# Attention scores of the last three row blocks of a four-layer graph network: from an element-wise product to a small matmul

## The chip, the cores and the metric

The kernel runs on one core of one Trainium2 chip. The metric is the device time of one execution in microseconds (us). TensorE (PE) does matmuls, VectorE (DVE), ScalarE (ACT) and GpSimd (POOL) work element by element, and SyncE (SP) issues most of the DMAs. Each engine runs its own instructions in the order of its own queue, and waits on semaphores for the others.

## The reference, cut to what matters

A graph of 2708 nodes with 512 features passes through four layers, each of the form x = x + layer(relu(layernorm(x)), adj). Layers 0, 1 and 3 aggregate over neighbours with the adjacency matrix. The change lies in layer 2, a graph attention layer with 8 heads of 64 outputs:

```
Wh = einsum('nd,hdo->hno', x, W)          # W: 8 x 512 x 64
f1 = einsum('hno,ho->hn', Wh, a1)
f2 = einsum('hno,ho->hn', Wh, a2)
e  = leaky_relu(f1[:, :, None] + f2[:, None, :], 0.2)
e  = where(adj > 0, e, -9e15)
h' = einsum('hnm,hmo->hno', softmax(e), Wh)
out = elu(h')
```

So every node has 16 scores: for each head the product of its 64 values Wh with a1 and with a2. Because Wh is itself x times W, a score is also x times a vector of 512 numbers: the sum over o of W[h, d, o] * a1[h, o].

## The kernel before

The nodes are cut into 22 chunks of 128 rows (R = 128, NC = 22; the last has 20 rows). All matmuls concerned are in fp32. All PSUM tiles come from one pool of eight banks, `ps`.

**Layer 1's aggregation** (`aggregate`, L433) runs over seven spans of chunks (4, 4, 4, 4, 3, 2 and 1 of them), and for each over the 22 blocks m of neighbours. For each pair, VectorE makes one tile of weights `kt` (`weight1`, L871, the instruction of L873), four units ahead of the matmuls (L425) that use it; `kt` has five buffers. In the middle of each span `before1` (L901) is called for each chunk c of the span, to load its rows.

**Layer 2's dense stage** is a pipeline over the chunks (`dense`, L271; `staged`, L251). For each chunk: load, normalize, transpose by TensorE into `hT` (L246, evicted by ScalarE at L248), then `product2` (L1104):

- TensorE multiplies `hT` with `w2s`, the weights of all heads, into `wh_ps` (L187; L200 for the last chunk), ScalarE copies it to `wh` (L1112, L1110), and SyncE stores it to DRAM (`whd`, L101).
- VectorE multiplies `wh` with the row of a1, GpSimd with the row of a2 (both L1117, output `wh_a`, four buffers). GpSimd then adds the upper half of each head's 64 products to the lower half (L1123).

One step later `sums2` (L1127) sums both products over o with two VectorE reductions (L1134), placed behind the next chunk's first product, and a VectorE instruction of 16 columns clamps the scores to +-31 and writes them to `f12` (L1136). The last stage, `rows2` (L1191), takes the scores of the first 11 chunks (in two groups) through exponentials and to DRAM as rows (`exps_nodes`, L1152, gives `er`; `exps2`, L1155, gives `ef` and `ec`; `row2`, L1145), and starts the attention: the broadcast row `rb` is loaded (L983) and the first weights are made.

**Attention** is a list of steps (unit, m); a unit is a head, or half the columns of the first and of the last head. Each step needs a tile `t` that VectorE makes from `rb`, `ec` and the adjacency (`make`, L1060, the instruction of L1070; four buffers, three steps ahead of use) and a tile `whs` that ScalarE scales (`scale`, L1045; L1054 and L1056; four buffers, three steps ahead too). TensorE then runs 16 matmuls into `av` and, where needed, 8 into `sums` (both L1318). A plan written out by hand (`behind`, L1423) adds to each step what else is due: the scores of chunks 11 to 21 through `exps_nodes` and `exps2` at step 4, their rows (TensorE transposes them into `f_ps` at L1147, ScalarE copies at L1149 and issues the store itself at L1150) from step 4 on, ScalarE's casts of the adjacency to bf16 (`mask`, L1382, tile `x`), TensorE's neighbour counts that use them (`count_neighbors`, L1394, `adj_sums`), small tiles for the 20 last rows (`load_tails`, L995), and the next layer's weights `wfs` and `wfn` (`load_l3_weights`, L1416), which take the two buffers of the pool `weights` that `w2s` and the score vectors `arows` (L1099) hold before.

The order of each engine's queue comes from a scheduler that merges these streams; `issue_after` places one instruction behind another.

Of the kernel before, what the change touches and what calls it, by code (L numbers as in the profile page):

```python
# [8 lines left out]
F32 = mybir.dt.float32  # L9
# [6 lines left out]
ALU = mybir.AluOpType  # L16
AX = mybir.AxisListType
# [3 lines left out]
P = 128  # L21

R = 128
# [15 lines left out]
F_MAX = 30.0  # L39
# [5 lines left out]
def fast_layers(  # L45
# [36 lines left out]
    nc = tc.nc  # L82
    N, D = x_in.shape
    H, _, O = w2.shape
    NC = -(-N // R)
    NF = D // P
# [5 lines left out]
    def rows(c):  # L92
        return min(R, N - c * R)

    def move(engine, dst, src):

        if dst.shape[0] == last_rows:
            cut = last_rows // 16 * 16
            engine.dma_start(dst[:cut], src[:cut])
            return engine.dma_start(dst[cut:], src[cut:])  # L100
        return engine.dma_start(dst, src)  # L101
# [8 lines left out]
    KMAX = max(sizes)  # L110
# [7 lines left out]
    const = ctx.enter_context(tc.tile_pool(name="const", bufs=1))  # L118
    small = ctx.enter_context(tc.tile_pool(name="small", bufs=4))
    weights = ctx.enter_context(tc.tile_pool(name="weights", bufs=2))  # L120
    dram = ctx.enter_context(tc.tile_pool(name="dram", bufs=1, space=DRAM))

    common = ctx.enter_context(tc.tile_pool(name="common", bufs=2))

    ps = ctx.enter_context(tc.tile_pool(name="ps", bufs=8, space=PSUM, reuse_waits="tile"))

    ident = const.tile([P, P], F32, name="ident")
    make_identity(nc, ident)
    oneb = const.tile([P, 32], BF16, name="oneb")
    nc.gpsimd.memset(oneb, 1.0)  # L130
    ones = const.tile([P, 1], F32, name="ones")
# [45 lines left out]
    def load_row(pool, src, name, into=None):  # L177

        t = into
        if t is None:  # L180
            t = pool.tile([P, D], F32, name=name)
        nc.sync.dma_start(t, bass.AP(tensor=src.tensor, offset=src.offset, ap=[[0, P], [1, D]]))
        return t
# [24 lines left out]
    def any_product(c, po, lhsT, w, n):  # L208
        if c == NC - 1:
            product_of_last(po, lhsT, w)  # L210
        else:
            product(po, lhsT, w, n)
# [106 lines left out]
    def load_x(src, c, name="x", pool=None, bufs=XBUFS, twice=False, tag=None, rows_of=natural):  # L319
        n = rows(c)  # L320
        t = (pool or common).tile([P, D], F32, name=name, tag=tag or name, bufs=bufs)
        if twice and c == NC - 1:
            nc.gpsimd.memset(t[:R], 0.0)
            move(nc.sync, t[TAIL : TAIL + n, :], rows_of(src, c))
        loads[c] = move(nc.sync, t[:n], rows_of(src, c)).ins
        return t
# [85 lines left out]
    def pattern(m, cs, n=R):  # L412

        g, k = where[m]
        v = vT[g][:n, k, cs[0] * R : (cs[-1] + 1) * R]
        return v.rearrange("p (c r) -> p c r", r=R)

    def by_chunk(t, cs):
        return t[:, : len(cs) * R].rearrange("p (c r) -> p c r", r=R)
# [56 lines left out]
    with ExitStack() as ring_ctx:  # L476
# [390 lines left out]
        w2s = weights.tile([P, NF, H, O], F32, name="w2s", tag="w")  # L867
        for f in range(NF):
            nc.sync.dma_start(w2s[:, f], w2[:, f * P : (f + 1) * P, :].rearrange("h p o -> p h o"))

        def weight1(m, cs):  # L871
            kt = wk.tile([R, WG], F32R, name="kt", bufs=5)
            nc.vector.scalar_tensor_tensor(  # L873
                by_chunk(kt, cs),
                lastr[:, cs[0] * R : (cs[-1] + 1) * R].rearrange("p (c r) -> p c r", r=R),
                index[:R, m : m + 1],
                pattern(m, cs),
                op0=ALU.is_ge,
                op1=ALU.mult,
            )  # L880
            return kt
# [17 lines left out]
        wmax = const.tile([P, 2], F32, name="wmax")  # L899

        def before1(c):  # L901
            if c == 2 * KMAX:
                for i, op in enumerate((ALU.max, ALU.min)):
                    nc.vector.tensor_reduce(
                        wmax[:, i : i + 1], w2s.rearrange("p f h o -> p (f h o)"), AX.X, op
                    )
            return load_x(x1, c)

        stages2 = dense(
            x2,  # L910
            lambda *args: product2(*args),
            False,
            [(3, lambda c: save_last2(c)), (4, lambda c: sums2(c)), (6, lambda c: rows2(c))],
            scalar=True,
        )
        ahead = [(m, emit_step, step, NC, stages2) for step, m in enumerate(AHEAD)]
        aggregate(weight1, h1, before1, after1, lead=4, ahead=ahead)


# [39 lines left out]
    f12 = late.tile([P, NC, 2 * H], F32, name="f12")  # L959
# [136 lines left out]

    l2p = ctx.enter_context(ExitStack())
    pp = l2p.enter_context(tc.tile_pool(name="l2p", bufs=2, side="right", reuse_waits="tile"))
    arows = weights.tile([P, NF, D], F32, name="arows", tag="w")  # L1099
    ar = [load_row(None, a, None, into=arows[:, i]) for i, a in enumerate((a1, a2))]  # L1100

    products, firsts = {}, {}

    def product2(c, xc, hT, n):  # L1104
        po = ps.tile([P, D], F32, name="wh_ps", tag="ps")
        any_product(c, po, hT, w2s.rearrange("p f h o -> p f (h o)"), n)
        wh = pp.tile([R, D], F32, name="wh", bufs=3)
        if c == NC - 1:
            for own in corners:
                nc.scalar.copy(wh[:n, own[1]], po[own])  # L1110
        else:
            nc.scalar.copy(wh[:n], po[:n])  # L1112
        move(nc.sync, whd[c * R : c * R + n, :], wh[:n])
        for i in range(2):
            t = products[c, i] = pp.tile([R, H, O], F32, name="wh_a", bufs=4)
            eng = nc.gpsimd if i else nc.vector
            ins = eng.tensor_tensor(  # L1117
                t[:n].rearrange("p h o -> p (h o)"), wh[:n], ar[i][:n], ALU.mult
            )
            if i == 0:  # L1120
                firsts[c] = ins.ins
            else:
                nc.gpsimd.tensor_tensor(  # L1123
                    t[:n, :, : O // 2], t[:n, :, : O // 2], t[:n, :, O // 2 :], ALU.add
                )

    def sums2(c):  # L1127
        n = rows(c)
        f = small.tile([P, 2, H], F32, name="f")

        with tc.issue_after(firsts[min(c + 1, NC - 1)]):
            for i in range(2):
                t = products.pop((c, i))
                nc.vector.tensor_reduce(f[:n, i, :], t[:n, :, : O // (1 + i)], AX.X, ALU.add)  # L1134

        nc.vector.tensor_scalar(  # L1136
            f12[:n, c, :],
            f[:n].rearrange("p i h -> p (i h)"),
            F_MAX + 1.0,
            -F_MAX - 1.0,  # L1140
            op0=ALU.min,
            op1=ALU.max,
        )

    def row2(c):  # L1145
# [4 lines left out]
        nc.scalar.dma_start(rT[:, c * R : (c + 1) * R], r)  # L1150

    def exps_nodes(cs):  # L1152
        nc.scalar.activation(er[:, cs], f12[:R, cs, :H], AF.Exp, scale=1.0 - SLOPE2)

    def exps2(cs):  # L1155
# [35 lines left out]
    def rows2(c):  # L1191
        for first, end in early_rows:
            if c == end - 1:
                exps_nodes(slice(first, end))
            for n in range(2):
                if first <= first + 2 * (c - end + 1) + n < end and c >= end - 1:
                    row2(first + 2 * (c - end + 1) + n)
        if c == EARLY - 1:
            exps2(slice(0, EARLY))
        if c == EARLY + 1:  # L1200
            load_row1(*units[0])
            split(0, EARLY)

        if c == LATE:
            load_wh(0)
            load_wh(GROUP)
        if LATE < c <= LATE + 3:
            scale(len(made))
            make(len(made))
# [213 lines left out]
    def behind(s, fn, *args):  # L1423
        plan.setdefault(s, []).append((fn, args))

    behind(4, exps_nodes, slice(EARLY, NC))
    behind(4, exps2, slice(EARLY, NC))
    for c in range(EARLY, NC):
# [755 lines left out]
def kernel(tc: tile.TileContext, *args: bass.AP):  # L2184

    nc = tc.nc
    with tc.tile_pool(name="verdict", bufs=1) as pool:
        verdict = pool.tile([1, 1], I32, name="verdict")
        fast_layers(tc, *args, verdict)
        odd = nc.values_load(verdict[0:1, 0:1], min_val=0, max_val=P + 1)  # L2190
        with tc.If(odd > 0):
            general_layers(tc, *args)
# [32 lines left out]
```

## Time and profile before

| what | value |
|---|---|
| time, three runs | 1741.11, 1741.48 and 1742.69 us; median 1741.48 |
| the profiled execution | 1741.66 us, of which the span from first to last instruction is 1739.8 us |
| TensorE busy | 1716.4 us (99% of the span) |
| VectorE, ScalarE, GpSimd busy | 75%, 49%, 14% |
| granted TensorE clock | 1.00 throughout |
| layer 1's aggregation | first matmul at 507.9 us |
| layer 2's dense stage | 725.4 to 810.1 us |
| attention's first matmul | 810.1 us |

A line of the timeline gives start, duration, engine, source line, operation, and output<-inputs; a number in brackets is the idle time of that engine just before, and what ended it. In the lines of windows each engine's busy time in the stretch stands with its number of instructions. An fp32 matmul shows as two records on TensorE. Matmuls overlap in their pipeline, so that the distance from one start to the next says more than a record's own duration.

### The profile page before, as it was taken

How to read it: one execution, taken by the hardware profiler on the slowest of the kernel's cores; microseconds unless marked ns; L12 is line 12 of the kernel's file. 1: busy time of each engine (PE TensorE's matmuls, PEld its weight loads, DVE VectorE, ACT ScalarE, POOL GpSimd, SP SyncE). 2: the span in 40 equal slices, each digit the busy share in tenths (PEclk: the TensorE clock that was granted, in tenths of full speed). 3: DMA queues.
4: the chain of work that ended last, by engine and by line, in shares of the span. 5: the costliest groups of instructions: out<-in, count | busy, mean ns of one | idle time of the engine just before them, and what ended most of it. 6: DMA issues, size and time to landing. Idle time of an engine off the chain costs nothing.

```text
span 1739.8 us, 29452 instructions
## 1 busy us (share of the span) xinstructions
PE 1716.4 (99%) x11280; PEld 1078.0 (62%) x11280; DVE 1309.3 (75%) x1902; ACT 846.7 (49%) x1556; POOL 248.5 (14%) x252
## 2 busy tenths in 40 slices
PE   8999999999999999999999999999999999999998
PEld 4567777744458888644575676434434455588886
DVE  7759889855555556888899999999999777633334
ACT  5446767622210000266878888888885666400000
POOL 1003323311111111366000000000001222100000
PEclk9999999999999999999999999999999999999999
DMA  8446666444551111332420220122022444313221
GB/s 288 140 124 195 204 207 190 141 116 123 123 142 49 49 49 49 117 129 99 118 79 15 61 64 26 47 65 63 16 69 70 142 140 130 106 40 106 74 73 41
DMA packets 167227, 177.37 MB, mean 102 GB/s; under 512 B 84127, under 2 KB 106591, under 8 KB 166060
## 3 DMA queue, kind: packets, MB, share of 16 engines
q1 hardware_dynamic: 144428, 131.99, 27.3%
q10 hardware_dynamic: 18808, 33.37, 5.1%
q0 software_dynamic: 3840, 10.03, 1.5%
q8 instruction: 90, 1.47, 0.4%
q14 instruction: 61, 0.50, 0.1%
HBM read 111.64 MB, written 55.36 MB: 96 GB/s over the span
## 4 chain that ended last, share of the span: by engine, by line
PE 87%; DVE 7%; ACT 2%; DMA 1%; issue 1%; SPq 1%; POOL 0%; ACTq 0%; DVEq 0%; POOLq 0%
PE acc L425 37%; PE av L1318 19%; PE nb_ps L187 8%; PE sums L1318 5%; PE h_ps L187 4%; PE self_ps L187 4%; PE line_ps L187 4%; DVE t L1070 4%; PE hT_ps L246 2%; PE fused_ps L371 2%; PE wh_ps L187 1%; DVE wh_a L1117 1%; PE av_ps L1253 1%; ACT b L1088 1%; DVE f L1134 1%
## 5 line engine op out<-in xcount | busy, mean ns | idle before, releaser
L1070 DVE SCALAR_TENSOR_TENSOR t<-rb,ec,vT 128x2708 f32<-128x2708 f32 (+2 forms) x214 | 510.7, 2447 | 8.1 <-PE sums L1318 6.3
L1318 PE MATMUL av<-t,whs 128*32 128x451 f32 (+5 forms) x4432 | 444.0, 513 | 5.9 <-DVE t L1070 4.6
L425 PE MATMUL acc<-halves,kt 128*128 128x512 f32 x1848 | 423.6, 390 | 1.0 <-DVE kt L873 1.0
L425 PEld LDWEIGHTS acc<-halves,kt 128*128 128x128 f32 x1848 | 346.0, 188 | 75.3 <-DVE kt L873 2.6
L1088 ACT ACTIVATE b<-t,eb 128x2708 bf16<-128x2708 f32 (+1 forms) x119 | 285.1, 2396 | 32.9 <-DVE t L1070 32.7
L1318 PEld LDWEIGHTS av<-t,whs 128*32 128x32 f32 (+1 forms) x4432 | 194.2, 110 | 163.1 <-issue 113.1
L425 PE MATMUL acc<-halves,ar 128*128 128x512 f32 x924 | 243.6, 414 | 0.0
L425 PEld LDWEIGHTS acc<-halves,ar 128*128 128x128 f32 x924 | 172.6, 188 | 58.2 <-issue 20.8
L223 ACT ACTIVATE ln_rs<-ln_mv,eps 128x1 f32<-128x1 f32 x88 | 25.8, 295 | 308.8 <-DVE ln_mv L221 307.3
L873 DVE SCALAR_TENSOR_TENSOR kt<-lastr,index,vT 128x512 fp32r<-128x512 int16 (+3 forms) x154 | 112.7, 746 | 72.3 <-PE acc L425 72.1
L1542 DVE CAST kt<-vT 128x512 fp32r<-128x512 uint8 (+3 forms) x154 | 56.3, 367 | 130.8 <-PE acc L425 130.7
L1270 POOL TENSOR_SCALAR z<-y 128x512 f32<-128x512 f32 x22 | 44.2, 2009 | 632.1 <-DVE y L1263 632.1
L558 DVE TENSOR_TENSOR_SCAN cum<-ai,deg 128x512 int16<-128x512 int32 (+2 forms) x110 | 128.1, 1168 | 0.0
L601 ACT ACTIVATE cum<-cum,limit 128x512 int16<-128x512 int16 (+3 forms) x132 | 88.0, 667 | 51.9 <-DVE deg L566 49.7
L1318 PE MATMUL sums<-t,whs 128*32 128x325 f32 (+4 forms) x952 | 103.5, 446 | 0.0
L1054 ACT ACTIVATE whs<-wh,ef 128x64 f32<-128x64 f32 x214 | 72.4, 341 | 53.4 <-PE av L1318 19.1
L219 DVE BATCH_NORM_STATS2 ln_st<-x 128x6 f32<-128x512 f32 x88 | 60.4, 688 | 48.6 <-DMA x<-x 34.4
L1318 PE MATMUL sums<-b,parts 128*32 128x338 bf16 (+2 forms) x884 | 77.1, 308 | 0.0
L187 PE MATMUL wh_ps<-w2s,hT 128*128 128x512 f32 x168 | 75.9, 594 | 0.6 <-ACT hT L248 0.6
L187 PE MATMUL h_ps<-w0s,hT 128*128 128x512 f32 x168 | 75.8, 594 | 0.1
L187 PE MATMUL self_ps<-wfs,hT 128*128 128x512 f32 x168 | 75.7, 593 | 0.0
L552 ACT ACTIVATE ar<-ai 128x512 fp32r<-128x512 int32 (+2 forms) x132 | 74.9, 568 | 1.4 <-DMA ai<-in_adj 0.9
(211 smaller groups left out, 1951.3 us busy)
## 6 DMA issues: line engine op xcount, KB each, us to landing
x<-x SPq DMA_DIRECT2D x105, 256.0 KB
ai<-in_adj SPq DMA_DIRECT2D x84, 256.0 KB
x<-x ACTq DMA_DIRECT2D x84, 256.0 KB
x<-in_x SPq DMA_DIRECT2D x42, 256.0 KB
rb<-rT SPq DMA_DIRECT2D x7, 1354.0 KB
wh<-whd SPq DMA_DIRECT2D x63, 96.0 KB
packed<-two POOLq DMA_DIRECT2D x44, 128.0 KB, 3.3
whd<-wh SPq DMA_DIRECT2D x21, 256.0 KB
```

The lines of the kernel that those rows point to most:

```text
L187: nc.tensor.matmul(po[:n], lhsT[:, f, :n], w[:, f, :], start=(f == 0), stop=(f == NF - 1))
L219: nc.vector.bn_stats(st[:n], xc[:n])
L425: nc.tensor.matmul(acc[:R], weight[:, k * R : (k + 1) * R], parts[:, i, :], start=(m == 0 and i == 0), stop=(m == NC - 1),)
L552: nc.scalar.activation(ar[:, :gw], ai[:, :gw], AF.Square, accum_out=squares[:R, m, g : g + 1])
L558: nc.vector.tensor_tensor_scan(cum[:n, :gw], ai[:n, :gw], ai[:n, :gw], 0.0 if g == 0 else deg[:n, m : m + 1], op0=ALU.add, op1=ALU.max,)
L601: nc.scalar.activation(cum[:n, :gw], cum[:n, :gw], AF.Sign, bias=limit[:n], scale=-1.0, accum_out=signs[:n, m, g : g + 1],)
L873: nc.vector.scalar_tensor_tensor(by_chunk(kt, cs), lastr[:, cs[0] * R : (cs[-1] + 1) * R].rearrange("p (c r) -> p c r", r=R), index[:R, m ...
L1054: ins = nc.scalar.activation(t[:q, :O], wh.pop((u, m))[:q], AF.Copy, scale=by)
L1070: ins = nc.vector.scalar_tensor_tensor(t[:q, : hi - lo], row[h][:q, lo:hi], ec[:q, m, h : h + 1], vT[g][:q, k, lo:hi], op0=ALU.max, op1=AL ...
L1088: nc.scalar.activation(b[:q, : hi - lo], weight[s][:, : hi - lo], AF.Sigmoid, bias=eb[:q, m, h : h + 1], scale=STEEP,)
L1318: nc.tensor.matmul(p[j * S : (j + 1) * S, : b - a], lhsT, rhs[:, part * size + a : part * size + b], start=(s % NC == 0), stop=(s % NC == ...
L1542: nc.vector.tensor_copy(by_chunk(kt, cs), pattern(m, cs))
```

## The change

- `arows` is loaded before layer 1's aggregation rather than at the start of layer 2.
- During layer 1's aggregation eight calls `fold(j)`, one from each of `before1(4)` to `before1(11)`, multiply `w2s` of one block of 128 input features with a1's or a2's row and sum over o, both on VectorE. This gives `w2a`, 512 x 16.
- For chunks 19, 20 and 21 (`DIRECT = NC - 3`) the scores are `hT` times `w2a`: four matmuls of 16 columns into a PSUM tile `fd_ps`, and one VectorE clamp from there to `f12`. The two products, GpSimd's addition and the two reductions fall away for them.
- For chunks 0 to 18 the reductions write to `f12` directly, and the clamp is done in place once for each group of chunks, in `exps_nodes`: chunks 0 to 5, 6 to 10, and 11 to 18.

```diff
+    w2a = const.tile([P, NF, 2 * H], F32, name="w2a")
...
+        arows = weights.tile([P, NF, D], F32, name="arows", tag="w")
+        ar = [load_row(None, a, None, into=arows[:, i]) for i, a in enumerate((a1, a2))]
+
+        def fold(j):
+            i, f = divmod(j, NF)
+            t = common.tile([P, D], F32, name="folded", tag="t", bufs=3)
+            nc.vector.tensor_tensor(
+                t, w2s[:, f].rearrange("p h o -> p (h o)"), ar[i], ALU.mult
+            )
+            nc.vector.tensor_reduce(
+                w2a[:, f, i * H : (i + 1) * H],
+                t.rearrange("p (h o) -> p h o", h=H),
+                AX.X,
+                ALU.add,
+            )
...
         def before1(c):
+            if KMAX <= c < KMAX + 2 * NF:
+                fold(c - KMAX)
...
-    arows = weights.tile([P, NF, D], F32, name="arows", tag="w")
-    ar = [load_row(None, a, None, into=arows[:, i]) for i, a in enumerate((a1, a2))]
-
+
+    DIRECT = NC - 3
     products, firsts = {}, {}
+
+    def direct(c, hT, n):
+        po = ps.tile([P, 2 * H], F32, name="fd_ps", tag="ps")
+        for f in range(NF):
+            nc.tensor.matmul(
+                po[:n], hT[:, f, :n], w2a[:, f], start=(f == 0), stop=(f == NF - 1)
+            )
+        bound(f12[:n, c], po[:n])
...
         move(nc.sync, whd[c * R : c * R + n, :], wh[:n])
+        if c >= DIRECT:
+            direct(c, hT, n)
+            return
         for i in range(2):
...
     def sums2(c):
         n = rows(c)
-        f = small.tile([P, 2, H], F32, name="f")
-
-        with tc.issue_after(firsts[min(c + 1, NC - 1)]):
+        if c >= DIRECT:
+            return
+
+        with tc.issue_after(firsts[min(c + 1, DIRECT - 1)]):
             for i in range(2):
                 t = products.pop((c, i))
-                nc.vector.tensor_reduce(f[:n, i, :], t[:n, :, : O // (1 + i)], AX.X, ALU.add)
-
+                nc.vector.tensor_reduce(
+                    f12[:n, c, i * H : (i + 1) * H], t[:n, :, : O // (1 + i)], AX.X, ALU.add
+                )
+
+    def bound(out, f):
         nc.vector.tensor_scalar(
-            f12[:n, c, :],
-            f[:n].rearrange("p i h -> p (i h)"),
-            F_MAX + 1.0,
-            -F_MAX - 1.0,
-            op0=ALU.min,
-            op1=ALU.max,
+            out, f, F_MAX + 1.0, -F_MAX - 1.0, op0=ALU.min, op1=ALU.max
         )
...
     def exps_nodes(cs):
+        own = f12[:R, cs.start : min(cs.stop, DIRECT)]
+        bound(own, own)
         nc.scalar.activation(er[:, cs], f12[:R, cs, :H], AF.Exp, scale=1.0 - SLOPE2)
```

## The prediction, made before the changed kernel was run

> **What bounds the kernel now.** I read the page first (totals), then the windows around layer 2, then the timelines of TensorE, VectorE and ScalarE there, and last the waits. TensorE is at 99%, so only its idle moments and its own work can move the end.
>
> ```profile
> PE 1716.4 (99%) x11280; PEld 1078.0 (62%) x11280; DVE 1309.3 (75%) x1902; ACT 846.7 (49%) x1556; POOL 248.5 (14%) x252
> ...
> 725.40:810.10 84.70, 84.15 (x274) 40.88 (x273) 68.96 (x155) 53.42 (x123) 52.30 (x44) 1.00 0.38 124
> 810.10:820.60 10.50, 7.99 (x110) 4.58 (x106) 9.61 (x19) 5.01 (x10) 8.29 (x7) 1.00 0.47 143
> 820.60:845.40 24.80, 21.97 (x272) 9.64 (x276) 20.65 (x18) 20.09 (x61) 0.00 (x0) 1.00 0.27 74
> 845.40:900.00 54.60, 54.01 (x803) 44.49 (x799) 50.74 (x37) 44.69 (x110) 0.00 (x0) 1.00 0.37 98
> ```
>
> First number after the comma is TensorE's busy time. The dense stage loses 0.55 us, the next 35 us lose 2.51 + 2.83 = 5.34 us, then TensorE is full again. These are the gaps, on TensorE:
>
> ```profile
> 817.38 0.71 PE L1394 MATMUL adj_sums<-x,parts 128*24 128x352 bf16 x6
> 820.61 1.39 PE L1318 MATMUL av<-t,whs 128*32 128x352 f32 x16 [2.51 <-DVE t L1070]
> ...
> 825.50 0.27 PE L1147 MATMUL f_ps<-ident,er 128*8 128x128 f32 x1 [0.49 <-ACT row L1149]
> ...
> 839.34 0.44 PE L1394 MATMUL adj_sums<-x,parts 128*24 128x325 bf16 x5 [1.53 <-ACT x L1382]
> ```
>
> The first waits for the tile of attention step 4, which VectorE makes late, behind the scores of the last chunks:
>
> ```profile
> 808.98 1.67 DVE L1070 SCALAR_TENSOR_TENSOR t<-rb,ec,vT 128x1408 f32<-128x1408 f32 x1
> 810.57 1.25 DVE L1136 TENSOR_SCALAR f<-f 128x16 f32<-128x16 f32 x1
> 811.74 0.68 DVE L1117 TENSOR_TENSOR wh_a<-wh,arows 128x512 f32<-128x512 f32 x1
> ...
> 818.55 0.41 DVE L1134 TENSOR_REDUCE f<-wh_a 20x8 f32<-20x256 f32 x1 [0.79 <-POOL wh_a L1123]
> 818.89 1.66 DVE L1070 SCALAR_TENSOR_TENSOR t<-rb,ec,vT 128x1408 f32<-128x1408 f32 x1
> ```
>
> The later two wait for ScalarE, which stood still for the same scores and then ran a chain of casts and rows:
>
> ```profile
> 820.67 0.28 ACT L1153 ACTIVATE er<-f 128x88 f32<-128x88 f32 x1 [3.81 <-DVE f L1136]
> ...
> 822.46 2.71 ACT L1382 CAST x<-vT 128x704 bf16<-128x704 uint8 x4
> 825.19 0.41 ACT L1149 COPY row<-f_ps 8x128 f32<-8x128 f32 x2
> ```
>
> **What the Trainium skill says.** "SBUF — State Buffer", section "Who interferes with whom": a VectorE operation with two SBUF inputs, or in a two-port mode, and a GpSimd operation that reads SBUF exclude each other for a whole instruction. The trace agrees: GpSimd's product takes 1.27 us alone and 2.57 us beside VectorE's `t`; the clamp of 16 columns takes 0.17 us alone and 1.25 us at 810.57. "TensorE: Matmul & The Clock Gate", section "LDWEIGHTS (loading the stationary operand)": a load costs its columns divided by 1.2 in ns, 107 for 128 columns; the four transposes at 1383.77 follow each other at 0.11 us, so the trace agrees. "ScalarE: Activation LUTs", section "What ACT_TABLE_LOAD costs": about 1283 ns; the trace shows 1.28 at 815.58.
>
> **The change, part by part.** The order within the queues is that of the built changed kernel; times are worked out from the rows of before.
>
> *Folding in layer 1, added on VectorE.* Eight products (0.68, row of L1117 at 811.74) and eight reductions (0.54, mean of L1134), 9.8 us in two bursts of four. In a burst each `kt` (0.75) is followed by two products or two reductions, so a unit costs up to 0.75 + 1.36 = 2.1 us where TensorE needs 1.81 (the spacing of `kt`, 559.86 to 561.67). The debt of a burst is about 4 x 0.75 + 4 x 1.22 - 4 x 1.81 = 0.6, at worst 1.3 us. VectorE idles 1.06 us before each `kt` there, waiting for TensorE to free one, and `kt` is finished about 6 us before its use (made 559.86, four units ahead). I take nothing; the cover is that lead. Without it the fold would cost its 9.8 us. GpSimd's additions of that layer come at the start of a span, the fold in its middle.
>
> *Direct scores, added on TensorE.* Twelve fp32 matmuls, 24 records, before attention's first matmul, so all on the path. Nearest row: `sums_ps` (L1249), a pair of records with 16 columns, starts at 1384.21 and the next matmul at 1384.35: 0.14 us a matmul. Four each for chunks 19 and 20: 2 x 0.56. For chunk 21 with 20 columns to load I estimate 0.3. Together 1.4 us. Bounds: 0.7 (half, if loads hide better), and 9.4 if nothing overlapped: 16 x (0.19 + 0.26) for load and matmul of L1249, and 8 x (0.10 + 0.18) for the smaller. Less than nothing is excluded: TensorE isn't idle there.
>
> *Last chunks' products, removed.* VectorE loses three products, six reductions and three clamps, and 3 x 2 operations of GpSimd go with their locks. After the `t` of step 3 stand only four clamps: three from PSUM, and one in place for chunks 11 to 18. VectorE's sequence from `rb`'s landing at 798.33, with GpSimd's locks counted in: two `t` with a GpSimd product between (to 802.9), GpSimd's addition and the product of chunk 17 (804.1), reductions (805.1), a `t` (806.7), GpSimd's product and the product of chunk 18 (808.6), four reductions (810.5), the `t` of step 3 (812.1), the clamps at 0.2 (812.9). The `t` of step 4 needs step 0's buffer and is ready at about 815.1 instead of 820.5.
>
> *TensorE then.* Its first attention matmul moves from 810.1 to 811.5. Steps 0 to 3 and the counts (1.78 a step; the next step could have started at 817.6 before) end at 819.0. Step 4 starts there instead of at 820.61: 1.6 us gained, 2.51 + 0.5 of stall against 1.4 of new work.
>
> *ScalarE then, where the stall goes.* The table load and two exponentials now stand ahead of step 4's `whs`. The exponential waits for the last clamp (812.9); queued behind it are `whs` and masks. None is late: `whs` needs step 0's end (813.7) anyway. ScalarE follows TensorE through steps 0 to 3, so the chain that began at 822.46 begins after step 3's end (819.1) and one `whs`: 819.55, 2.9 us earlier. The rows begin at 822.3, TensorE's `f_ps` at 820.9, and the wait of 0.49 falls away. But the chain is as long as before: from 822.46 to 839.2, 16.7 us with two casts, row copies, and stores that it issues itself. TensorE reaches the counts of 837.49 at 834.5, ScalarE is ready at 836.2. What is late next is thus still ScalarE, and everything from there on is earlier by its 2.9 to 3.1 us, not by more.
>
> *SyncE and the buffers.* `arows` now frees first, so four loads of `wfs` stand ahead of the stores of chunks 19 to 21, waiting for chunk 18's products (808.6); `wfn` follows, waiting for the end of `w2s` (811), and no longer stands behind the tails. The delayed stores are read at step 18 and later, and by the tails, which follow the `wh` load that waits for step 5's `whs` (816.0): they start at 816.4 instead of 818.99, 2.6 us earlier, less than the 2.9 of ScalarE. The last `tails_v` (835.23 before) shares a wait with the row store at 838.03; one load stands before it less, so it too comes about 3 us earlier. I count 0, with -1 to +1.7 kept.
>
> *Group clamps.* Sixteen small instructions less on VectorE in the dense stage, where TensorE is full; 0 to 0.5 us (its two idle moments wait for ScalarE). Taken: 0.1.
>
> *After 845 us* TensorE is full and VectorE waits for it, so a shift there reaches the end. Sum: -3.0 - 0.1 = -3.1 us. Against the profiled execution's 1741.66 us (span 1739.8 and 1.9 around it) that is 1738.6; that execution lies 0.2 above the median of 1741.48, so I predict 1738.4.
>
> **The rivals.** *All waits vanish.* If ScalarE's chain gets shorter too (its issues wait for DMAs of the tails), the gain is all idle time, 5.34, and the stretched `f_ps` pairs (0.61, 0.68 and 0.53 in the timeline at 827.88, 830.34 and 833.12, against 0.38 unhindered: 0.7), less 1.4: 4.6 us, 1736.9. For it: about 4 us of that chain are waits; against: those DMAs move along with it. *ScalarE's chain stretches.* Eight weight loads of 256 KB now fall ahead of the tails and rows rather than half of them after; if small DMAs queue behind them, the chain gives back 1.8 us: 1740.2. For it: DMA share is 0.47 at 810 to 820 already; against: 2 MB at the 143 GB/s shown are 15 us from 809 and rows begin at 822. *The direct matmuls don't overlap:* 9.4 us before attention, place as above. Step 4 then starts at 827 instead of 820.6 and ScalarE's chain at 827.55 instead of 822.46: 5.1 us slower, 1746.6. It decides from 4.3 us of direct matmuls (2.9 + 1.4), 0.18 per record, where the pair at 1384.21 shows 0.07.
>
> **How the numbers follow.** Likeliest case 0.52, all waits vanish 0.20, stretch 0.23, no overlap 0.05. A measurement tells about 0.2% (3.5 us, 1738.0) from no change. Two fifths of the likeliest case (its spread is about 1 us) and nearly all of the second lie below: 0.40 faster. The rest of the first and the third: 0.54 same. Slower 0.06. The range from 1736.4 to 1740.7 leaves out the last case and the outer parts of the second and third.
>
> **What would show it.** `fd_ps` starts 0.14 apart by matmul; the idle of 2.51 for `t` gone; attention's first matmul about 1.4 us later and step 4 about 1.6 earlier; the 3.81 on ScalarE gone; a wait of 1 to 2 us at the counts of step 10 still there; no new wait for `kt`. A changed wait at the counts, or `fd_ps` at 0.3 a matmul, would make me wrong.

## The result, and the profile after

| kernel | time, median (us) | against the kernel before on the same chip |
|---|---|---|
| before | 1742.10 (13 runs, 1740.71 to 1744.01) | |
| changed | 1738.93 (13 runs, 1737.64 to 1740.22) | 0.9982, 95% interval 0.9975 to 0.9989 |
| changed, measured again beside later experiments | 1739.09 (11 runs); before there 1743.02 (33 runs) | 0.9978, 0.9969 to 0.9987 |

So the change takes 3.2 us off, and 3.9 in the second measurement; 3.1 were forecast. The first profiled execution of the changed kernel took 1739.97 us (span 1738.2), the second 1739.33 (span 1737.5).

The page's totals and the windows of the first one (dense stage; attention's steps 0 to 3; steps 4 to about 14; the rest of that stretch). The first three edges lie at the same events as before, the last two, 845.40 and 900, at the same times. First number after the comma: TensorE's busy time.

```profile
PE 1718.7 (99%) x11304; PEld 1074.6 (62%) x11304; DVE 1310.7 (75%) x1893; ACT 846.7 (49%) x1556; POOL 239.9 (14%) x246
...
724.89:810.86 85.97, 85.97 (x301) 43.30 (x300) 67.69 (x145) 53.41 (x123) 52.06 (x44) 1.00 0.39 130
810.86:818.27 7.41, 7.41 (x114) 3.46 (x112) 5.23 (x5) 6.27 (x18) 0.00 (x0) 1.00 0.79 251
818.27:845.40 27.13, 24.67 (x317) 11.34 (x309) 19.16 (x16) 21.53 (x63) 0.00 (x0) 1.00 0.26 62
845.40:900.00 54.60, 54.18 (x790) 35.52 (x786) 51.85 (x38) 43.62 (x101) 0.00 (x0) 0.97 0.33 93
```

TensorE has 24 instructions more, VectorE nine fewer, GpSimd six fewer. The dense stage is full now (85.97 of 85.97), but longer than the 84.70 of before; steps 0 to 3 take 7.41 us rather than 10.50 and contain no idle time. Of the 5.34 us that TensorE stood still after them, 2.46 are left. TensorE's timeline shows the new matmuls and where those 2.46 are:

```profile
803.29 0.96 PE L1125 MATMUL fd_ps<-w2a,hT 128*128 128x16 f32 x8
...
810.70 0.33 PE L1125 MATMUL fd_ps<-w2a,hT 128*20 128x16 f32 x7
...
818.27 1.38 PE L1348 MATMUL av<-t,whs 128*32 128x352 f32 x16
...
836.46 0.44 PE L1424 MATMUL adj_sums<-x,parts 128*24 128x325 bf16 x5 [1.68 <-ACT x L1412]
...
841.84 0.30 PE L1424 MATMUL adj_sums<-x,parts 128*24 128x325 bf16 x1 [0.62 <-ACT x L1412]
```

Step 4 (818.27) has no bracket any more. The wait at the counts of step 10 is still there, 1.68 us against 1.53. On VectorE the products and reductions of the last three chunks are gone; after the `t` of step 3 stand four clamps only:

```profile
808.16 1.67 DVE L1089 SCALAR_TENSOR_TENSOR t<-rb,ec,vT 128x1408 f32<-128x1408 f32 x1
809.75 0.16 DVE L1169 TENSOR_SCALAR f<-fd_ps 128x16 f32<-128x16 f32 x1
809.84 0.21 DVE L1169 TENSOR_SCALAR f<-f 128x128 f32<-128x128 f32 x1
...
811.09 0.16 DVE L1169 TENSOR_SCALAR f<-fd_ps 20x16 f32<-20x16 f32 x1 [0.96 <-PE fd_ps L1125]
```

and on ScalarE the exponential of the scores begins at 813.01 rather than 820.67, with no idle time before it:

```profile
813.01 0.28 ACT L1183 ACTIVATE er<-f 128x88 f32<-128x88 f32 x1
...
818.72 2.71 ACT L1412 CAST x<-vT 128x704 bf16<-128x704 uint8 x4
821.46 0.41 ACT L1177 COPY row<-f_ps 8x128 f32<-8x128 f32 x2
821.74 1.58 ACTq L1178 DMA_DIRECT2D rT<-row  x2
823.37 0.35 ACT L1073 ACTIVATE whs<-wh,ef 128x64 f32<-128x64 f32 x1 [1.50 <-issue]
```

The chain that began at 822.46 begins at 818.72. The last two lines show ScalarE held for 1.50 us by two row stores that it issues itself; the same pair took 0.81 us before, and 1.19 in the changed kernel's second profile.

The first product of the dense stage starts at 725.42 us before, and at 724.89 and 725.91 in the two profiles of the changed kernel. So I compare distances between events rather than moments. In us, from the starts on TensorE (D: first matmul of the dense stage to that of chunk 19; A: from there to attention's first matmul; then attention's steps 0 to 3, 4 to 10, 11 to 29; last column: D to step 30 in all):

```
                          D       A     0-3    4-10   11-29   D to step 30
before                  75.86    8.83  10.50  18.89   38.01   152.09
changed                 74.96   11.01   7.41  18.35   39.17   150.90
changed, second profile 74.98   11.00   7.41  18.08   38.03   149.51
predicted change        -0.1    +1.4   -3.0   -1.4     0       -3.1
```

From step 30 to the end it is 862.1 to 862.4 us in all three. The 39.17 contains a dip of the clock: in that execution the granted clock fell at 860 us, as the windows show (clock: third number from the end).

```profile
858.00:860.00 2.00, 1.63 (x24) 0.36 (x12) 1.47 (x2) 1.61 (x6) 0.00 (x0) 1.00 0.09 23
860.00:862.00 2.00, 1.96 (x20) 0.84 (x24) 2.00 (x2) 2.00 (x6) 0.00 (x0) 0.59 0.58 144
862.00:864.00 2.00, 2.00 (x26) 0.98 (x22) 2.00 (x2) 2.00 (x6) 0.00 (x0) 0.55 0.34 82
```

It cost 1.1 us (39.17 against 38.03). Without it the two profiles give -2.3 and -2.6 us.

### The profile page after: what moved, and what is told of

Its sections match the earlier page's. It is cut to its first block, busy times and chain, and to the rows that moved or that the text cites. A ratio compares the mean times of both kernels' runs of the same rounds, so it can differ in the third digit from the quotient of the medians.

```text
span 1738.2 us, 29482 instructions
## 1 busy us (share of the span) xinstructions
PE 1718.7 (99%) x11304; PEld 1074.6 (62%) x11304; DVE 1310.7 (75%) x1893; ACT 846.7 (49%) x1556; POOL 239.9 (14%) x246
## 4 chain that ended last, share of the span: by engine, by line
PE 89%; DVE 6%; issue 2%; ACT 1%; SPq 1%; DMA 0%; DVEq 0%; ACTq 0%
PE acc L426 37%; PE av L1348 17%; PE nb_ps L188 8%; DVE t L1089 5%; PE h_ps L188 4%; PE wh_ps L188 4%; PE self_ps L188 4%; PE line_ps L188 4%; PE sums L1348 4%; PE hT_ps L247 2%; PE fused_ps L372 2%; ACT b L1107 1%; PE av_ps L1283 1%; DMA ws<-in_L_gnn_W_self 0%; PE sums_ps L633 0%
```

## The experiments

In the expectations theory 1 is the prediction's likeliest case: ScalarE's chain, with the row stores that it issues, sets the end of steps 4 to 10. Its rivals are that transfers (tails, rows, weights) set it, and others that each expectation names. Experiments are built from the changed kernel; ratios are against the kernel before on the same chip, and columns are those of the table above.

```
                        median  ratio   95% interval        D       A     0-3    4-10   11-29   D to step 30
group clamps alone      1742.24 1.0004  0.9996 to 1.0012  74.97    8.82   9.88  19.94   39.04   152.64
direct scores alone     1738.73 0.9983  0.9975 to 0.9991  75.91   11.00   7.41  17.78   38.01   150.12
direct matmuls twice    1740.08 0.9990  0.9982 to 0.9998  74.97   12.99   7.41  17.20   38.01   150.59
two direct chunks       1740.20 0.9992  0.9984 to 1.0000  74.98   10.21   7.41  19.15   38.72   150.46
rows by GpSimd          1737.43 0.9972  0.9961 to 0.9983  74.78   11.01   7.41  17.23   37.74   148.16
late weights            1738.01 0.9974  0.9964 to 0.9984  75.08   11.01   7.41  17.80   38.01   149.31
rows + two direct       1739.36 0.9986  0.9980 to 0.9993  74.98   10.21   7.41  18.04   38.97   149.61
no fold                 1738.58 0.9980  0.9972 to 0.9988  75.08   11.01   7.41  18.35   39.18   151.03
rows + late             1738.93 0.9978  0.9969 to 0.9986  74.98   11.01   7.41  17.30   39.29   149.99
rows + late + two       1739.23 0.9976  0.9967 to 0.9985  75.05   10.21   7.41  17.82   38.67   149.16
two direct + late       1738.58 0.9974  0.9965 to 0.9983  74.78   10.21   7.41  17.78   38.29   148.48
```

In the column of steps 11 to 29, no fold and the one with all three edits contain the dip of the clock; elsewhere a value off 38.0 means that waits at the counts were moved across step 11.

**1. Group clamps alone.**

```diff
-    DIRECT = NC - 3
+    DIRECT = NC
...
-            if KMAX <= c < KMAX + 2 * NF:
-                fold(c - KMAX)
```

> Group clamps alone, without folding and without direct scores: all 22 chunks take the two products. Theory 1 (the last chunks' products make the tile of step 4 and ScalarE's exponentials late; direct scores cost TensorE 1.9 us and give back about 4): the dense stage still loses its two waits for hT (about 0.7 us earlier), but the tile of step 4 still comes behind GpSimd's last products (idle of about 2 us stays), and since the clamp of chunks 11 to 21 now stands behind three tiles, ScalarE's exponentials come 2 to 3 us later than before and the wait at the counts of step 10 grows by as much: 0 to 2 us slower than before in all. Theory 2 (fewer small VectorE instructions in the dense stage carry the gain): about 3 us faster than before, as the whole change.

Measured 1742.24 us, no different from before (ratio 1.0004, against 0.9982 for the whole change). But D is 0.89 shorter: the dense stage's gain belongs to this part. It is given back later: the clamp of chunks 11 to 21 in one piece must wait for the last chunk's sum, so the exponential comes at 821.86 rather than 820.67. TensorE's waits:

```profile
818.52 1.39 PE L1346 MATMUL av<-t,whs 128*32 128x352 f32 x16 [1.89 <-DVE t L1087]
...
822.18 0.38 PE L1173 MATMUL f_ps<-ident,er 128*8 128x128 f32 x2 [1.11 <-ACT er L1181]
```

The idle time for `t` remains, and a new one of 1.11 for the exponential stands behind it. Alone, this part is worth nothing that the times show.

**2. Direct scores alone** (a clamp per chunk as before).

```diff
+        bound(f12[:n, c], f12[:n, c])
...
-        own = f12[:R, cs.start : min(cs.stop, DIRECT)]
-        bound(own, own)
```

> Folding and direct scores for the last three chunks as in the change, but chunks 0 to 18 are clamped one by one as before. Theory 1: the direct matmuls take 1.9 us of TensorE, the idle of 2.5 us before step 4 is gone, the wait at the counts of step 10 stays at 1 to 2 us; the dense stage keeps its two waits for hT (0.19 and 0.36): about 2.4 us faster than before, 0.7 slower than the whole change. Theory 2: no gain left, within 0.5 us of before.

Measured 1738.73 us, the whole of the change's gain. D is back at 75.91 and TensorE's two waits in the dense stage are back:

```profile
765.20 3.70 PE L188 MATMUL wh_ps<-w2s,hT 128*128 128x512 f32 x8 [0.20 <-ACT hT L249]
793.74 3.70 PE L188 MATMUL wh_ps<-w2s,hT 128*128 128x512 f32 x8 [0.41 <-ACT hT L249]
```

Steps 4 to 10 are shorter in exchange (17.78 against 18.08 and 18.35). In the profiles the group clamps are still worth 0.6 us to step 30 (150.12 against 149.51); the medians don't tell the two kernels apart.

**3. Direct matmuls twice.**

```diff
-        for f in range(NF):
+        for f in (*range(NF), *range(NF)):
```

> The whole change, with the direct matmuls done twice into the same accumulator (24 rather than 12, same values). If their time lies wholly on the path (theory 1): attention's first matmul comes 1.9 us later than in the change, ScalarE's chain starts with it, and the whole is 1.9 us slower than the change, 1.2 us faster than before. If the end of the stretch is set by transfers of SyncE and not by TensorE (theory 3): the wait at the counts of step 10 shrinks from 1.68 to near 0, and the time stays within 0.5 us of the change.

A grows by 1.99 us, which is the price of a series of twelve once more. Of that 1.15 reach the median (1.08 the profile, against the second one of the changed kernel). The rest goes into the waits at the counts, which shrink from 1.79 and 0.64 to:

```profile
832.40 0.27 PE L1175 MATMUL f_ps<-ident,er 128*8 128x128 f32 x1 [0.24 <-ACT row L1177]
...
837.60 0.44 PE L1424 MATMUL adj_sums<-x,parts 128*24 128x325 bf16 x5 [0.76 <-ACT x L1412]
...
841.87 0.44 PE L1424 MATMUL adj_sums<-x,parts 128*24 128x325 bf16 x4 [0.25 <-ACT x L1412]
...
842.97 0.30 PE L1424 MATMUL adj_sums<-x,parts 128*24 128x325 bf16 x1 [0.19 <-ACT x L1412]
```

2.43 before, 1.44 now: 1.0 us of 2.0 is absorbed. So a second series of direct matmuls is half hidden by ScalarE's lateness, which theory 1 had not allowed for (it expected the whole to show) and its rival had allowed too much for.

**4. Two direct chunks.**

```diff
-    DIRECT = NC - 3
+    DIRECT = NC - 2
```

> The whole change with direct scores for chunks 20 and 21 alone; chunk 19 takes the two products again. Theory 1: TensorE loses 0.9 us less to direct matmuls; VectorE's tile of step 4, which was ready 3.6 us ahead of its use, comes about 2.5 us later (a product, two reductions, GpSimd's locks) and is still in time: 0.9 us faster than the change, 4 faster than before. If the margin is smaller than that: an idle of up to 1 us before step 4 comes back and the gain is lost. Theory 3: as the change.

A miss: A is 0.79 shorter and step 4 still has no idle time, but the median is 1.3 us above the changed kernel's, not below it (the intervals of the ratios overlap, and the profile is 0.95 us longer to step 30). Steps 4 to 10 take 19.15: TensorE's waits in steps 4 to 13 come to 3.50 us, against 2.43 in the second profile of the changed kernel, and 2.12 of them are new ones for rows. SyncE's queue, of the changed kernel:

```profile
806.47 1.74 SPq L175 DMA_DIRECT2D wfs<-fused  x4
...
816.07 0.83 SPq L1023 DMA_DIRECT2D tails_v<-vT  x1
```

and of this one:

```profile
810.70 2.71 SPq L175 DMA_DIRECT2D wfs<-fused  x4
...
817.20 0.83 SPq L1023 DMA_DIRECT2D tails_v<-vT  x1
```

The score vectors are needed for one chunk more, their buffer comes free 4.2 us later, the weight loads that wait for it hold the queue, and the tails start 1.1 us later although TensorE is ahead. That this lateness is what costs became theory 4, tried in experiment 10.

**5. Row stores issued by GpSimd.**

```diff
-        nc.scalar.dma_start(rT[:, c * R : (c + 1) * R], r)
+        eng = nc.gpsimd if c >= EARLY else nc.scalar
+        eng.dma_start(rT[:, c * R : (c + 1) * R], r)
```

> The changed kernel, but the stores of the rows of chunks 11 to 21 are issued by GpSimd rather than by ScalarE (ten of them lie in the chain that begins at 818.72 us). Theory 1 (ScalarE's own chain, with the issues that it makes itself, sets the end of the stretch): ten issues of 0.4 to 1.6 us leave the chain, the waits at the neighbour counts (1.68 and 0.62 us) shrink or vanish, and the kernel is 1.5 to 2.3 us faster than the changed one. Rival (the chain waits for the transfers themselves, wherever they are issued): the waits stay within 0.5 us of what they were, and the time too.

Measured 1737.43 us, 1.5 below the changed kernel's first median and 4.6 below the kernel before. TensorE's waits in steps 4 to 12, all of them:

```profile
827.92 0.27 PE L1175 MATMUL f_ps<-ident,er 128*8 128x128 f32 x1 [0.20 <-ACT row L1177]
831.42 0.27 PE L1175 MATMUL f_ps<-ident,er 128*8 128x128 f32 x1 [0.84 <-ACT row L1177]
840.14 0.30 PE L1425 MATMUL adj_sums<-x,parts 128*24 128x325 bf16 x1 [0.44 <-ACT x L1413]
840.78 0.44 PE L1425 MATMUL adj_sums<-x,parts 128*24 128x325 bf16 x5 [0.34 <-ACT x L1413]
```

The 1.68 at the counts of step 10 is gone, and the sum is 1.82 rather than 2.30: 0.78 at the counts, and 1.04 at rows that the changed kernel did not have. Steps 4 to 29 take 54.97 us, against 56.11 in the second profile of the changed kernel. This fits theory 1, at the low end of its numbers, and not the rival, that waits and time stay wherever the stores are issued. The times do not settle it: the interval of the ratio overlaps with the changed kernel's. Against the kernel of experiment 11, which was measured on the same chip, the median is 1.15 lower. This is what the Trainium skill says in "DMA: Bandwidth & Descriptors", section "Issuing engines are not separate DMA queues": a second issuing engine saves only the sequencer time of the issue. Here that time is 0.27 to 0.88 us for a store or a pair, and 1.58 and 1.19 for the first pair in the two profiles of the changed kernel, on the engine that TensorE waits for; on GpSimd, which is idle there, one takes 0.50.

Two things blur it. Two of ScalarE's row copies now wait for the transfers of earlier rows (0.52 and 0.69 us). And with the stores gone, ScalarE's queue was put in another order, and the tails' exponentials (L1032, at 851.38 in the changed kernel) came at 837.13. Here their data had arrived; in experiments 7 and 8 it had not.

**6. Layer 3's weights late.** The eight loads wait for a small VectorE instruction at step 30.

```diff
-            l3_weights.append(load_weight(weights, fused[i], name, tag="w"))
+            w = weights.tile([P, NF, D], F32, name=name, tag="w")
+            nc.vector.memset(w[:, :, :1], 0.0)
+            for k in range(NF):
+                nc.sync.dma_start(w[:, k], fused[i][k * P : (k + 1) * P, :])
+            l3_weights.append(w)
```

> The changed kernel, but the eight loads of layer 3's weights (2 MB, wfs and wfn) wait for a small VectorE instruction that comes at step 30 of the attention, so that they neither stand ahead of the tails nor share the DMA engines with the rows. Theory 1 (these loads stretch the two row issues at 821.7 to 0.8 us more than before): ScalarE's chain ends 0.8 us earlier, the wait at the counts of step 10 falls from 1.68 to about 0.9, and the time is 0.8 us lower than the changed kernel's. Rival (the stretch comes from the tails, which move along): wait and time as in the changed kernel, within 0.3 us.

The wait at the counts of step 10 falls to 1.03, as expected, and the pair of row stores takes 1.11 us, not 1.58; but in the second profile of the changed kernel it took 1.19 with the loads in their old place. A wait of 0.52 comes in at a row of step 8, and to step 30 only 0.2 us are left (149.31 against 149.51). The median is 0.9 lower than the first and 1.1 lower than the second of the changed kernel, across chips; by ratio (0.9974 against 0.9982 and 0.9978) the intervals overlap. So it is not shown that the loads stretch the chain; the profiles leave room for some tenths of a microsecond.

**7. Row stores by GpSimd and two direct chunks** (the edits of 4 and 5).

> The changed kernel with the direct scores for the last two chunks only, and the row stores issued by GpSimd. Theory 1: two direct chunks alone gained nothing more because ScalarE's chain kept its end; with the stores off that chain the 0.8 us of TensorE work saved come through, and the kernel is 2 to 3 us faster than the changed one. Rival (the transfers set the end): as the changed kernel, within 0.5 us.

A miss for theory 1: 1739.36 us, where 2 to 3 below the changed kernel was expected. ScalarE meets the exponentials that had moved up in its queue before the tails, which start at 817.81 here, have landed:

```profile
837.35 0.20 ACT L1032 ACTIVATE tails_f<-tails_f 120x1 f32<-120x1 f32 x1 [1.18 <-DMA tails_v<-vT]
...
838.38 0.78 ACT L1034 ACTIVATE tails_w<-tails_w,tails_f 120x576 f32<-120x576 f32 x1 [0.74 <-DMA tails_w<-one]
```

Its 1.92 us there are what TensorE then waits for at the counts (0.83 + 0.54 + 0.34). So with the issues off ScalarE, and in the order that its queue then has, the tails become the late one, which is the rival's mechanism.

**8. Row stores by GpSimd and late weights** (the edits of 5 and 6).

> The changed kernel with the row stores issued by GpSimd and layer 3's eight weight loads behind step 30. Theory 1 (ScalarE's own issues and the weight loads each lengthen the chain, at different places): the gains of the two edits alone (1.5 and 0.9 us) add to about 2 us below the changed kernel. Rival (both free the same wait): as with the row stores alone, 1.5 us below.

Neither came: 1738.93 us, no better than the changed kernel, and the profile 0.5 us longer. The exponentials moved up even further, ahead of the casts for the counts, and ScalarE stood before them:

```profile
837.50 0.20 ACT L1032 ACTIVATE tails_f<-tails_f 120x1 f32<-120x1 f32 x1 [2.47 <-issue]
```

Two edits that each free the chain don't add here, because the order that came out with both placed a wait in front of it, by my reading for the tails. The profile says "issue" for that wait; I take it from SyncE's last tails, whose last issue took 1.59 us from 834.79.

**9. All three edits** (4, 5 and 6).

> As the kernel before in this list, and direct scores for the last two chunks only. Theory 4 (with two direct chunks the score vectors' buffer comes free 4 us later, the weight loads that wait for it hold SyncE's queue, and the tails behind them start 1.1 us later; that ate the gain): without the loads ahead of the tails the tails start as early as with three direct chunks, and the 0.8 us of TensorE's work saved come through, so 0.5 to 1 us below the kernel before in this list. Rival (VectorE's later scores are what costs): as slow against its neighbour as before, 1.3 to 1.9 us above.

Inconclusive. (The kernel before in that list is the one of experiment 8.) The median is 0.3 above experiment 8, the profile 0.8 below it, with another dip of the clock inside (step 22 takes 2.74 us, not 2.17). Neither shows the rival's 1.3 to 1.9, and neither shows that the saving of 0.8 comes through.

**10. Two direct chunks and late weights** (the edits of 4 and 6).

> The changed kernel with two direct chunks and layer 3's loads behind step 30; the row stores stay on ScalarE. Theory 4: at or below the changed kernel with late loads (0.9 us under the changed one), down to 0.8 us less. Rival (ScalarE's chain and VectorE's later scores set it): at the time of two direct chunks alone, 1.3 us above the changed kernel.

1738.58 us, ratio 0.9974 (0.9965 to 0.9983), against 0.9992 (0.9984 to 1.0000) for two direct chunks alone: the loss of experiment 4 is gone. SyncE's tails:

```profile
812.81 0.83 SPq L1023 DMA_DIRECT2D tails_v<-vT  x1
816.24 0.39 SPq L1059 DMA_DIRECT2D wh<-whd  x1
816.72 0.76 SPq L1024 DMA_DIRECT2D tails_f<-f  x1
```

D to step 30 is 148.48 us, 1.0 below the second profile of the changed kernel and 2.0 below two direct chunks alone; the ratio equals that of late weights with three. ScalarE's waits for what SyncE loads (`wh`, `tails_w`) fall from 2.30 us in experiment 4 to 0.53; those for its own rows stay (3.31 and 2.79). So theory 4 holds: it was the weight loads and not VectorE's later scores. That they act through SyncE's queue is what the two timelines say; the edit also takes their 2 MB off the DMA engines in that stretch, and nothing here separates the two.

**11. No fold.** The scores of chunks 19 to 21 are not the reference's here: plain elements of W stand in the place of the folded vectors.

```diff
-            t = common.tile([P, D], F32, name="folded", tag="t", bufs=3)
-            nc.vector.tensor_tensor(
-                t, w2s[:, f].rearrange("p h o -> p (h o)"), ar[i], ALU.mult
-            )
-            nc.vector.tensor_reduce(
-                w2a[:, f, i * H : (i + 1) * H],
-                t.rearrange("p (h o) -> p h o", h=H),
-                AX.X,
-                ALU.add,
-            )
+            nc.vector.tensor_copy(w2a[:, f, i * H : (i + 1) * H], w2s[:, f, :, i])
```

> The changed kernel without the folding: in its place a VectorE copy of eight columns puts two plain elements of W into the tile, so the scores of chunks 19 to 21 are not those of the reference; all else is left. Prediction's step (the fold is free behind the lead of the weight tiles): same time as the changed kernel, within 0.3 us, and attention begins at the same moment after layer 1's start. Rival (VectorE's debt in the two bursts reaches TensorE, or the shared memory port slows its neighbours): 0.6 to 1.3 us faster than the changed kernel.

1738.58 us, ratio 0.9980 against 0.9982: the fold is free within what can be measured. Attention's first matmul comes 303.68 us after the first one of layer 1's aggregation, and 303.56 with the fold. Where its time comes from is seen in the waits before `kt` of the changed kernel (us, times):

```profile
  PE acc L426: 193.6, 186
...
  PEld acc L426: 3.5, 7
```

VectorE's idle time while TensorE frees a `kt` is 193.6 us against 202.8 before and 202.5 without the fold: the fold used some 9 of it. TensorE's waits for `kt` stay at 3.5.

**12. The changed kernel again.**

> The changed kernel once more, beside the three others on the same chip, with a second profile. If the dip of the clock at 860 to 864 us was chance, step 22 of the attention takes 2.17 us rather than 2.96 and the span is about 1 us shorter than in its first profile; if the kernel brings it, it is there again. Time as in its first measurement, 3.2 us below the kernel before, within 0.7.

The dip of the clock is not there (step 22 takes 2.16 us), so the kernel doesn't bring it every time. Of the profiles made here, three show it at this place: this kernel's first, experiment 11's and experiment 9's. The other columns of the table repeat within 0.3 us. The time is 3.9 us below the kernel before, at the edge of what was expected.

But for group clamps alone, no kernel here is set apart from the changed one by its interval. The row stores by GpSimd come nearest: 0.9961 to 0.9983, the lowest median of all.

## Why the prediction was right

Its total was right, and the place: what was late on VectorE went away, ScalarE was late next, and the wait at the counts set how much was left. The terms were not all right: the gain of the clamps and the cost of the direct matmuls were each taken 0.8 us too small, and that these two errors cancelled is luck.

- *Group clamps, 0.1 (up to 0.5).* Too small for the dense stage: 0.9 us (experiments 1 and 2), of which the profiles keep 0.6 to step 30. The prediction called the dense stage's two idle moments waits for ScalarE, and so out of the clamps' reach. That it was the clamps, the two experiments show. The way is my reading and not shown: ScalarE itself waited for VectorE's statistics, one step upstream, and the clamps stood in that queue. ScalarE's wait for one chunk's statistics, between the two idle moments, before:

```profile
770.04 0.29 ACT L223 ACTIVATE ln_rs<-ln_mv,eps 128x1 f32<-128x1 f32 x1 [0.71 <-DVE ln_mv L221]
```

  and with the change:

```profile
768.94 0.29 ACT L224 ACTIVATE ln_rs<-ln_mv,eps 128x1 f32<-128x1 f32 x1 [0.40 <-DVE ln_mv L222]
```

  Both idle moments went. They also had cost more than the 0.55 us of their brackets: the two matmuls behind them came 0.8 us earlier.
- *Direct matmuls, 1.4.* Too small: 2.2 us in A (and 1.99 for the series repeated in experiment 3), 0.89 for a full chunk (803.29 to 804.18), 0.16 for the last. The step that failed is the choice of a row: a single pair of records, 0.14 us apart from the next matmul, for a series in which every record loads 128 columns of `hT`. The prediction had the right price at hand. By the Trainium skill's "TensorE: Matmul & The Clock Gate", section "LDWEIGHTS (loading the stationary operand)", at 107 ns a load, eight loads are an estimated 0.86 us; the trace agrees with 0.89. In this series the records follow each other at 0.11 us with 128 columns to load and at 0.02 us with 20, so the loads set the pace. Half of such a cost, added once more, was hidden by the wait at the counts (experiment 3).
- *The stall at step 4, 3.0.* Right: 3.09 in steps 0 to 3, in every kernel with direct scores.
- *ScalarE's chain, 2.9 earlier, no shorter.* The start came 3.2 us earlier in the distances above, `f_ps`'s wait of 0.49 went, the counts' wait stayed (1.68). But the chain got longer, so that steps 4 to 10 gained 0.5 to 0.8 us where 1.4 were worked out. In ScalarE's lines the first pair of row stores takes 1.58 us (1.19 in the second profile) where it took 0.81, beside a `tails_v` of 1.39 (1.00) on SyncE, and its waits for the tails come to 2.15 (2.25) where they were 1.89. That is a stretch such as the second rival had, at some 0.6 to 0.9 us instead of 1.8, but its mechanism is not shown: the DMA share is 0.93 at 814 to 816 us and only 0.04 to 0.18 from 818 to 826, so the weight loads are mostly past when these stores are issued, and with the loads late the pair still takes 1.11 (experiment 6).
- *SyncE, 0.* The tails started at 816.07 for 816.4 worked out. Counting the queues one by one was worth it: experiment 4 shows what 1.1 us of lateness there does.
- *Fold, 0.* Right (experiment 11).
- *After 845 us, nothing.* Right.

Sum in the profiles: -0.9 + 2.2 - 3.1 - 0.5 to -0.8 is -2.3 (first profile, the clock's 1.1 us left out) and -2.6 us (second), less than the -3.1 of the prediction; the medians say -3.2 and -3.9. The remaining 0.9 and 1.3 us are not located, so the agreement of 3.1 with 3.2 to a tenth is luck too. The one profiled execution of before took 1741.66 us, 0.4 below the median of the first comparison; the changed kernel's took 1739.97, 1.0 above its own. Two single executions can hide that much, so the profiles settle where the time went and the medians how much.

There is one lead. The profiled execution of before had a mean granted clock of 1.000. The 116 others of that kernel whose clock is on record had 0.997 to 0.999, 94 of them 0.998 or less; of the changed kernel's 24, 7 had 0.998 and 17 had 0.999. Among the fourteen profiles 0.998 goes with the dip at 860 us. So the kernel before may meet such a dip more often than its one profile says, and the changed one less often. It is a lead only: on two of the three chips the executions of before with 0.999 are no faster than those with 0.998, and group clamps alone, at 0.999 and 1.000, gained nothing.

*All waits vanish* was wrong by the 2.30 us still there at the counts. *No overlap* was wrong by its own point: 0.11 us a record, not 0.18.

## What to carry to other kernels

Price a series of small matmuls by its weight loads, not by one pair that could hide behind a neighbour; and when an idle moment is put down to an engine, ask what that engine had waited for before deciding that another engine's saving can't reach it. When a stall is removed, work out the next late chain with every issue that its engine makes itself: moving those issues to an idle engine gave the lowest median of all, 1.5 us below the changed kernel's, though the intervals overlap. And look at who holds a buffer that a queued load waits for: needing one tile for one more chunk held SyncE's queue for 4 us.

## What the runs showed that was not expected

- A row store issued by ScalarE takes 0.27 us in most cases. The second of the first pair met a load that SyncE issued at the same moment: it took 1.22 us in the first profile of the changed kernel and 0.83 in the second, and the load 1.39 and 1.00 instead of 0.71. By GpSimd a store takes 0.50 to 0.53 throughout.
- The granted clock of a kernel on one core can fall to 0.50 for about 3.4 us (860.4 to 863.8 in the first profile of the changed kernel, in windows of 0.5 us) although TensorE had stood still for only 0.42 us just before. It did so at one place of the program in three profiles out of thirteen with parts of the change, and in one of the two of the changed kernel itself. In all fourteen, that of before too, it also falls at the very end, after TensorE's last matmul.
- A TensorE wait shown as 0.36 us (before, at 793.43) moved the next start by 0.52: from one chunk's product to the next it took 4.39 us rather than 3.87.
